# Degrees of a batch as a stream of their own, one batch ahead, in a four-layer graph kernel

## The chip, the cores and the metric

The kernel runs on one core of a Trainium2 chip. A core has a TensorE for matrix products (PE in the profile; PEld is its weight load), VectorE (DVE), ScalarE (ACT), GpSimd (POOL) and SyncE (SP), which here only starts transfers. SBUF is the memory on the core, PSUM holds the results of TensorE, and DMA engines move data between them and the chip's main memory. The metric is the time on the device in microseconds, as the median of several runs.

## The reference

The input is 16 graphs (batches) of 1024 nodes with 128 features and a symmetric 0/1 adjacency of 1024 x 1024. Four residual layers follow one another. The change lies in the second, a three-layer GraphSAGE on a thinned ("dilated") adjacency:

```python
def _sage(x, adj, Wr, Wx, b, mf):
    deg = jnp.clip(jnp.sum(adj, axis=-1, keepdims=True), 1.0, None)
    agg = jnp.einsum('bij,bjd->bid', adj, x) / deg
    out = agg @ Wr + x @ Wx + b
    nrm = jnp.maximum(jnp.linalg.norm(out, axis=-1, keepdims=True), NORM_EPS)
    return out / nrm * mf[..., None]
...
adj_d = _dilate(adj, mask)
h1 = _bn(jax.nn.relu(_sage(x, adj_d, Wr1, Wx1, b1, mf)), g1, be1)
h2 = _bn(jax.nn.relu(_sage(h1, adj_d, Wr2, Wx2, b2, mf)), g2, be2)
h3 = _bn(jax.nn.relu(_sage(h2, adj_d, Wr3, Wx3, b3, mf)), g3, be3)
```

`_bn` takes mean and variance over all batches and nodes, so that every layer must be done with all 16 batches before the next begins. `deg`, the number of neighbours of each node, is the same in the three layers; the kernel computes its reciprocal once, in the first of them, which the code calls layer 1 (`l == 0`).

## The kernel before

The kernel has one stage per part: attention with layer norm, the thinning of the adjacency (to about 990 us), the three GraphSAGE layers, and the last two residual layers. The stage of the change is layer 1, from 990 to about 1350 us. Three names need a word. In the profile the 8-bit adjacency is `carry` (the resident copies of the batches 8 to 15) or `A` (the copies `A8` of the batches 0 to 7, loaded again from main memory, four buffers). `d` stands for both d16 and d8, `step` for the constant matrix of twos.

A batch goes through three generators in the class `Step`, each of which yields where another may take over.

- `first(b)` begins with the degrees: `degree_product` (L1281) multiplies the adjacency by a matrix of twos, 8 blocks times 4 quarters, 32 matmuls, each quarter in a 32-column tile of TensorE's array. ScalarE copies the four quarters of the sums into `row` (L1397, one partition, 2 KB). GpSimd starts a transfer that folds the row into 8 partitions, d16 (L1399). VectorE takes a minimum for a later flag (L1400), halves the sums and clips them at 1 (L1402) and takes reciprocals (L1403). GpSimd writes them to main memory (L1404), and SyncE loads them spread over all 128 partitions as `rdeg` (L1389, 512 KB). Of `row`, d16 and d8 there is one buffer each, of `rdeg` there are three. Then `first` transposes x (L759), splits it into two float32r parts `hi` (ScalarE, L1272) and `lo` (VectorE, L1273, one buffer), widens the adjacency into 8 pieces `a` (ScalarE L1295, VectorE L1293, 8 buffers), multiplies in two halves of 16 matmuls each (L1306) and scales each half by `rdeg` into `ag` (L1416).
- `out(b)` multiplies by the weights (L1432, 16 float32 matmuls, which the profile shows as 32), adds the bias (L1435), squares (L1442), sums (L1443), takes a power on GpSimd (L745) and scales the rows (L1451, L1457).
- `keep(b)` transposes the result (L759), takes statistics (L1471), writes it out (L1474), and already makes layer 2's adjacency product of that batch, with a second split, a second set of pieces and 32 matmuls (L1306), scaled by `rdeg` into `ag` (L1483), which is written out (L1486).

`load(b)` (L1369, L1372) brings A8 and x.

What order do they come in? `take_turns` advances a list of streams one yield at a time. For the i-th of the 16 batches of the layer's order, the list holds `load` of batch i+2, `first` of i+1, `out` of i and `keep` of i-1. I call one round of the list a turn. The framework then arranges the instructions of each engine itself, so the built order differs from the written one. In the built program the degree product stands in two blocks a turn: 20 matmuls after the first 38 of the turn's 64 adjacency matmuls (the 32 of `keep` and the first 6 of the 32 of `first`), where `lo` of `first` is made, and 12 after the last of them. [...]

Of the kernel before, what the change touches and what calls it, by code (L numbers as in the profile page):

```python
# [639 lines left out]
def fast_kernel(ctx: ExitStack, tc: tile.TileContext, t: dict, out: bass.AP, flag: bass.AP):  # L640

    nc = tc.nc
    B, N, D = t["x"].shape
# [110 lines left out]
    def turned(psum, src, tag="h"):  # L754

        for p, c, blocks in halves(psum, tag):
            for i, k in enumerate(blocks):
                s = src[:, k, :] if len(src.shape) == 3 else src[:, k * P:(k + 1) * P]
                nc.tensor.transpose(p[:, i * P:(i + 1) * P], s, identf)  # L759
            yield p, c, slice(blocks[0], blocks[-1] + 1)  # L760
# [50 lines left out]
    def take_turns(streams):  # L811
        while streams:
            streams = [s for s in streams if next(s, streams) is not streams]
# [41 lines left out]
    step = consts.tile([P, P + 512 + P], BF16, name="step")  # L855
# [168 lines left out]
    for b in range(1, B):  # L1024
        streams = []
# [8 lines left out]
    with ExitStack() as ph:  # L1034
# [142 lines left out]
        for i in range(1, len(steps) + 1):  # L1177
            streams = [fixed_point(*steps[i])] if i < len(steps) else []
# [79 lines left out]
    with ExitStack() as ph:  # L1258
# [9 lines left out]
        def split(n):  # L1268

            hi = work.tile([P, NT, P], F32R, name="hi")  # L1270
            lo = work.tile([P, NT, P], F32R, name="lo", bufs=1)
            nc.scalar.copy(hi, n)  # L1272
            nc.vector.tensor_sub(lo, n, hi.bitcast(F32))  # L1273
            return hi, lo

        def degree_product(A):

            acc = ps_a.tile([P, 512], F32, name="acc")
            for jt in range(NT):
                for q in range(4):  # L1280
                    nc.tensor.matmul(acc[32 * q:32 * q + 32, :N // 4], twos[:, :32], A[:, jt, q * N // 4:(q + 1) * N // 4],  # L1281
                                     start=(jt == 0), stop=(jt == NT - 1), tile_position=(0, 32 * q))
            for q in range(4):
                yield acc[32 * q:32 * q + 1, :N // 4], slice(q * N // 4, (q + 1) * N // 4)

        def widened(A):

            for h in range(H2):
                c = slice(h * 512, (h + 1) * 512)
                for i in range(NT // 2):  # L1290
                    a = wide_pool.tile([P, 2, 512], F32R, name="a", bufs=NT)
                    if i % 2:
                        nc.vector.tensor_copy(a, A[:, 2 * i:2 * i + 2, c])  # L1293
                    else:
                        nc.scalar.copy(a, A[:, 2 * i:2 * i + 2, c])  # L1295
                    yield a

        def adjacency_product(pieces, parts):

            for h in range(H2):  # L1300
                acc = ps_a.tile([P, 512], F32, name="acc")
                late = 0 if h else 1
                for i in range(NT // 2 + late):
                    for part, k in zip(parts, (i, i - late)):
                        for jt in range(2 * k, 2 * k + 2) if 0 <= k < NT // 2 else ():
                            nc.tensor.matmul(acc, part[:, jt, :], pieces[h * NT // 2 + k][:, jt - 2 * k, :],  # L1306
                                             start=(part is parts[0] and jt == 0), stop=(part is parts[1] and jt == NT - 1))
                yield acc, slice(h * 512, (h + 1) * 512)
# [6 lines left out]
        class Step:  # L1315
# [73 lines left out]
                nc.sync.dma_start(st.rdeg, bass.AP(tensor=rdeg_d[b].tensor, offset=rdeg_d[b].offset,  # L1389
                                                   ap=[[0, P], [1, N]]))  # L1390

            def first(self, b):

                st = self.batches[b]
                row = work.tile([1, N], F16, name="row", bufs=1)
                for acc, c in degree_product(st.A):
                    nc.scalar.copy(row[:, c], acc)  # L1397
                d16 = small.tile([NT, P], F16, name="d16", bufs=1)
                nc.gpsimd.dma_start(d16, row)  # L1399
                nc.vector.tensor_reduce(nodeg[:NT, b:b + 1], d16, AX.X, OP.min)  # L1400
                d8 = small.tile([NT, P], F32, name="d8", bufs=1)
                nc.vector.tensor_scalar(d8, d16, 0.5, 1.0, op0=OP.mult, op1=OP.max)  # L1402
                nc.vector.reciprocal(d8, d8)  # L1403
                nc.gpsimd.dma_start(rdeg_d[b], d8)  # L1404
                self.load_rdeg(b)
                yield
                st.hT = work.tile([P, N], F32, name="hT")
                for p, c, _ in turned(ps_h, st.x):
                    nc.scalar.copy(st.hT[:, c], p)
                yield  # L1410
                parts = split(st.x)
                pieces = list(widened(st.A))
                yield
                st.ag = work.tile([P, N], F32, name="ag", bufs=3)
                for acc, c in adjacency_product(pieces, parts):
                    nc.vector.tensor_mul(st.ag[:, c], acc, st.rdeg[:, c])  # L1416
                    yield
# [74 lines left out]
        order = [*range(B // 2, B), *range(B // 2)]  # L1492

        lag = 0, 0, 1
        for l in range(3):
            step = Step(l, before)
            if l:
                before.norm()
                step.take_norm()
            if l == 2:  # L1500
                order = [b for pair in zip(order[:B // 2], order[B // 2:]) for b in pair]
            if l == 2:
                take_turns(left)
                left = []
            lead = 0 if l == 1 else 1
            take_turns([step.load(b) for b in order[:1 + lead]])
            if l == 0:
                take_turns([step.first(order[0])])
            outs = [step.out(b) for b in order]
            for i in range(B + lag[l]):  # L1510
                streams, left = left, []
                if i + 1 + lead < B:
                    streams.append(step.load(order[i + 1 + lead]))
                if l == 0 and i + 1 < B:
                    streams.append(step.first(order[i + 1]))
                kept = [step.keep(order[i - 1 - lag[l]])] if i > lag[l] else []
                if l == 2:
                    streams += kept
                if i < B:
                    streams.append(outs[i] if l < 2 else islice(outs[i], 2))  # L1520
                if l == 2 and i:
                    streams.append(outs[i - 1])
                if l < 2:
                    streams += kept
                take_turns(streams)
                if l == 2 and i == 0:

                    wide_ctx.close()
                    l2 = Layers23()
                elif l == 2 and i == B - 4:  # L1530
                    l2.weights(ps_h)
                elif l == 2 and i == B - 3:
                    l2.load(l2.state[0], 0)

            rest = step.keep(order[B - 1])
            next(rest)
            left = [rest]
            before = step
# [7 lines left out]
    with ExitStack() as ph:  # L1546
# [257 lines left out]
        for b in range(B - 1):  # L1804
            streams = []
# [31 lines left out]
def kernel(tc: tile.TileContext, t: dict, out: bass.AP):  # L1837
    nc = tc.nc
    with tc.tile_pool(name="flag", bufs=1) as pool:
        flag = pool.tile([1, 1], I32, name="flag")  # L1840
        fast_kernel(tc, t, out, flag)
        with tc.If(nc.values_load(flag[0:1, 0:1]) != 0):
            general_kernel(tc, t, out)
# [22 lines left out]
```

## Time and profile before

| | |
|---|---|
| Median of 3 runs | 2682.58 us (2681.59 to 2685.39) |
| Profiled execution, its time | 2682.24 us |
| Its span in the profile | 2680.4 us |
| TensorE busy | 2521.3 us, 94% |
| VectorE busy | 2102.6 us, 78% |
| ScalarE busy | 1969.3 us, 73% |
| GpSimd busy | 330.8 us, 12% |

The span is what the profile covers; the time of an execution is a little longer. A row of the timeline has the start, the duration, the engine, the line, the operation with output and inputs, and in brackets the idle time of the engine just before it and what ended it. "<-issue" means that the engine waited for nothing that the profile shows. A row of the waits names the waiting engine and line, what it waited for, and then total, number and longest. In a row of stretches each engine has its busy time and, in brackets, its instructions.

### The profile page before, as it was taken

The numbers are of one execution on the slowest core, as the hardware profiler recorded it, in microseconds if no ns is written. First come the engines' busy times: TensorE is split into PE (matmuls) and PEld (weight loads), VectorE is DVE, ScalarE is ACT, GpSimd is POOL, SyncE is SP. The second block draws the span as 40 slices with busy tenths as digits, with TensorE's granted clock in tenths as the row PEclk, the third lists the DMA queues.
The fourth block names the chain that finished last, engine by engine and source line by source line (L and its number), as shares of the span: only waits on it lengthen the run. The fifth ranks groups of instructions, "written<-read, shape, count | busy, mean of one in ns | idle before, by whom it ended". The sixth has DMA issues, their size and how long they took to land.

```text
span 2680.4 us, 44092 instructions
## 1 busy us (share of the span) xinstructions
PE 2521.3 (94%) x16136; PEld 1800.2 (67%) x16136; DVE 2102.6 (78%) x5830; ACT 1969.3 (73%) x3172; POOL 330.8 (12%) x300
## 2 busy tenths in 40 slices
PE   7999999997889879999999998999999999999986
PEld 5667777765666658887788895466666666666655
DVE  6888888987898867777778875777878787887885
ACT  7898889886888776666555534777777777777773
POOL 0001111103000002111122232001101000001010
PEclk9999999998999989999999998999999999999998
DMA  5555545520000052233366672112221111111100
GB/s 193 181 176 171 173 161 174 179 96 21 2 3 2 1 221 90 100 111 134 133 241 236 211 283 111 40 38 73 74 91 64 64 63 63 63 63 63 48 24 26
DMA packets 109187, 285.59 MB, mean 107 GB/s; under 512 B 12192, under 2 KB 52128, under 8 KB 101792
## 3 DMA queue, kind: packets, MB, share of 16 engines
q1 hardware_dynamic: 87776, 196.58, 21.7%
q0 software_dynamic: 21184, 86.09, 8.8%
q8 instruction: 129, 2.11, 0.3%
q14 instruction: 98, 0.80, 0.1%
HBM read 202.78 MB, written 79.82 MB: 105 GB/s over the span
## 4 chain that ended last, share of the span: by engine, by line
PE 52%; DVE 19%; ACT 11%; issue 8%; POOL 4%; DMA 3%; POOLq 0%; ACTq 0%; DVEq 0%; SPq 0%
PE ph L1618 8%; PE acc L1678 7%; PE acc L1306 7%; PE ph L766 6%; PE ph L1432 4%; PE ph L759 3%; PE pmm L1690 3%; PE acc L973 2%; PE pmm L724 2%; ACT em L985 2%; PE ph L1605 2%; ACT xn L801 2%; DVE mid L1096 2%; DVE keep L1147 2%; POOL ln_rstd L745 2%
## 5 line engine op out<-in xcount | busy, mean ns | idle before, releaser
L973 PEld LDWEIGHTS acc<-hs,em 128*128 128x128 f32 x2048 | 248.7, 192 | 37.9 <-issue 26.8
L973 PE MATMUL acc<-hs,em 128*128 128x128 f32 x2048 | 269.1, 279 | 0.7 <-DVE hs L989 0.3
L1678 PE MATMUL acc<-ex,hs 128*128 128x512 f32 x512 | 248.9, 596 | 7.4 <-DVE hs L1705 4.5
L724 PE MATMUL pmm<-xT,G 128*128 128x512 f32 x512 | 251.4, 604 | 1.4 <-DVE mx L983 0.7
L801 ACT ACTIVATE xn<-xn,ln_nb,ln_rstd 128x128 f32<-128x128 f32 x512 | 204.7, 480 | 55.9 <-DVE ln_nb L799 55.8
L1306 PE MATMUL acc<-a,hi 128*128 128x512 f32 x768 | 233.6, 398 | 11.1 <-DVE a L1293 8.0
L1306 PE MATMUL acc<-a,lo 128*128 128x512 f32 x768 | 229.6, 393 | 5.8 <-DVE lo L1273 5.8
L745 POOL TENSOR_TENSOR ln_rstd<-ln_rstd,mhalf 128x8 f32<-128x8 f32 (+1 forms) x68 | 108.3, 1593 | 969.2 <-DVE ln_rstd L742 513.4
L983 DVE CUSTOM_DVE_ANT_0 em<-pmm,msk 128x1024 f32<-128x1024 f32 x128 | 155.9, 1218 | 35.1 <-PE pmm L724 32.8
L985 ACT ACTIVATE em<-em,mx 128x1024 f32<-128x1024 f32 x128 | 146.0, 1141 | 48.2 <-DVE mx L983 46.5
L1698 ACT ACTIVATE ex<-em,mn 128x1024 f32<-128x1024 f32 x128 | 146.9, 1147 | 45.0 <-DVE mn L1695 44.0
L1690 PE MATMUL pmm<-G,hT 128*128 128x512 f32 (+3 forms) x416 | 175.3, 523 | 0.1
L1695 DVE CUSTOM_DVE_ANT_0 em<-pmm,msk 128x1024 f32<-128x1024 f32 x128 | 155.4, 1214 | 24.5 <-PE pmm L1692 22.3
L1306 PEld LDWEIGHTS acc<-a,hi 128*128 128x128 f32 x768 | 142.2, 189 | 42.4 <-DVE a L1293 10.6
L1306 PEld LDWEIGHTS acc<-a,lo 128*128 128x128 f32 x768 | 143.5, 189 | 40.2 <-DVE lo L1273 10.5
L1156 ACT ACTIVATE carry<-pc,negone 128x1024 fp8e4<-128x1024 f32 x128 | 141.3, 1115 | 26.7 <-PE pc L1155 23.8
L931 ACT ACTIVATE carry<-an 128x1024 fp8e4<-128x1024 f32 x128 | 134.1, 1049 | 23.9 <-DMA an<-in_adj 23.3
L980 ACT ACTIVATE msk<-carry,l0nbig 128x1024 bf16<-128x1024 fp8e4 x128 | 145.9, 1140 | 0.0
L1686 ACT ACTIVATE msk<-A,nbig 128x1024 bf16<-128x1024 fp8e4 x128 | 144.3, 1138 | 0.0
L1618 PE MATMUL ph<-A,hi 128*128 128x512 f32 x512 | 143.2, 420 | 0.8 <-DVE zn L1607 0.6
L1678 PEld LDWEIGHTS acc<-ex,hs 128*128 128x128 f32 x512 | 88.6, 190 | 76.8 <-issue 54.7
L1295 ACT CAST a<-A 128x1024 fp32r<-128x1024 fp8e4 x96 | 98.4, 1048 | 54.5 <-PE acc L1306 53.4
(317 smaller groups left out, 6186.6 us busy)
## 6 DMA issues: line engine op xcount, KB each, us to landing
an<-in_adj SPq DMA_DIRECT2D x128, 512.0 KB, 4.1
adj_d<-carry POOLq DMA_DIRECT2D x16, 1024.0 KB, 4.6
A<-dil_d SPq DMA_DIRECT2D x16, 1024.0 KB, 5.6
rdeg<-rdeg_d SPq DMA_DIRECT2D x32, 512.0 KB, 3.8
A<-adj_d SPq DMA_DIRECT2D x16, 1024.0 KB, 4.8
ag_d<-ag POOLq DMA_DIRECT2D x24, 512.0 KB, 5.4
ag<-ag_d SPq DMA_DIRECT2D x24, 512.0 KB, 5.5
x_d<-xn POOLq DMA_DIRECT2D x16, 512.0 KB, 3.9
```

What stands on the lines that cost most here:

```text
L724: nc.tensor.matmul(p[:, h * 512:(h + 1) * 512], lhsT, rhs[:, h * 512:(h + 1) * 512], start=True, stop=True)
L745: nc.gpsimd.tensor_tensor(r, r, mhalf[:, :n], op=OP.pow)
L766: nc.tensor.matmul(p, W, x[:, c], start=(i == 0), stop=(i == len(pairs) - 1))
L801: nc.scalar.activation(r[:, k.start + i, :], r[:, k.start + i, :], AF.Identity, scale=rstd[:, i:i + 1], bias=nb[:, i:i + 1])
L973: nc.tensor.matmul(s.acc[:, c], em[:, c], hs, start=(jt == 0 and k % 4 == 0), stop=(jt == NT - 1 and k % 4 == 3))
L983: nc.vector.tensor_tensor_reduce(em, e, msk, 1.0, 3.0e38, op0=OP.add, op1=OP.min, accum_out=mn)
L985: nc.scalar.activation(em, em, AF.Exp, scale=-1.0, bias=mn, accum_out=sm)
L1306: nc.tensor.matmul(acc, part[:, jt, :], pieces[h * NT // 2 + k][:, jt - 2 * k, :], start=(part is parts[0] and jt == 0), stop=(part is par ...
L1618: nc.tensor.matmul(p, part[:, jt, :], A[jt][:, c], start=(jt == 0 and i == 0), stop=(jt == NT - 1 and i == 1))
L1678: nc.tensor.matmul(s.acc[:, c], hs, ex[:, c], start=(jt == 0), stop=(jt == NT - 1))
L1690: nc.tensor.matmul(e[:, c], s.hT[:, js], s.G[:, c], start=True, stop=True)
L1695: nc.vector.tensor_tensor_reduce(row, e, msk, 1.0, 0.0, op0=OP.add, op1=OP.min, accum_out=mn)
```

## The change

The degrees leave `first` and become a generator of their own, `degrees`, with two empty yields ahead of the product, one after the row's transfer and one at the end. `first` begins with the load of `rdeg`. Ahead of the loop the degrees of the first two batches are made; in the loop, `degrees` of batch i+2 is the last stream of the turn. The computation is the same.

```diff
-            def first(self, b):
+            def degrees(self, b):
 
                 st = self.batches[b]
+                yield
+                yield
                 row = work.tile([1, N], F16, name="row", bufs=1)
                 for acc, c in degree_product(st.A):
                     nc.scalar.copy(row[:, c], acc)
                 d16 = small.tile([NT, P], F16, name="d16", bufs=1)
                 nc.gpsimd.dma_start(d16, row)
+                yield
                 nc.vector.tensor_reduce(nodeg[:NT, b:b + 1], d16, AX.X, OP.min)
                 d8 = small.tile([NT, P], F32, name="d8", bufs=1)
                 nc.vector.tensor_scalar(d8, d16, 0.5, 1.0, op0=OP.mult, op1=OP.max)
                 nc.vector.reciprocal(d8, d8)
                 nc.gpsimd.dma_start(rdeg_d[b], d8)
+                yield
+
+            def first(self, b):
+
+                st = self.batches[b]
                 self.load_rdeg(b)
                 yield
...
             if l == 0:
-                take_turns([step.first(order[0])])
+                take_turns([chain(step.degrees(order[0]), step.first(order[0])), step.degrees(order[1])])
...
                 if l < 2:
                     streams += kept
+                if l == 0 and i + 2 < B:
+                    streams.append(step.degrees(order[i + 2]))
                 take_turns(streams)
```

In the order of the built program (the profile of before numbers the lines; in the changed file they are up to 10 higher), one turn of TensorE now runs: 16 adjacency matmuls of `keep`, all 32 of the degree product, 4 of `first`, 16 of `keep`, 2 of `first`, 2 of L1432, 7 transposes, 26 of `first`, 14 of L1432, the rest of the transposes. On VectorE, L1400, L1402 and L1403 stand directly ahead of `lo` of `first`; before, they stood among L1435, L1471 and L1443. From layer 2 on, the built order of every engine is the same in both.

## Prediction

> **What bounds the kernel now.** TensorE is busy 94% of the 2680.4 us span, and the change touches one stage only, layer 1 of the three inner graph layers. So I read that stage: busy time over stretches first, then who waits for whom there, then the chain of waits and the timeline of single turns. The stretches are cut at the starts of `keep`'s adjacency product (L1306), one per turn: 1023.58 for the first, 1197.04 for the ninth, 1314.96 for the fourteenth.
>
> ```profile
> core 0: us, PE busy (x) PEld busy (x) DVE busy (x) ACT busy (x) POOL busy (x), PEclk, DMA share, GB/s
> 1023.58:1197.02 173.44, 171.79 (x1155) 142.61 (x1154) 132.17 (x215) 117.58 (x162) 34.35 (x40) 1.00 0.29 102
> 1197.02:1315.22 118.20, 109.23 (x724) 89.04 (x723) 82.49 (x135) 73.77 (x102) 22.40 (x25) 1.00 0.37 131
> ```
>
> Eight turns take 21.68 us each with TensorE 99% busy; the next five take 23.58 with it 92% busy. The clock is 1.00 in both, so the 1.9 us between them is waiting. Who waits (1000 to 1330 us; total, times, longest):
>
> ```profile
> DVE nodeg L1400 <- DMA d<-row: 14.8, 6, 2.7
> ...
> PEld acc L1306 <- DVE a L1293: 10.6, 6, 2.0
> ...
> PEld L1281 <- issue: 9.9, 28, 0.4
> ```
>
> Six times VectorE stands at L1400 until the transfer of the degree row lands, and six times TensorE waits for a widened piece `a` that VectorE makes later. The timeline of the ninth turn has both (`d` is d16 and d8, `A` is the copy A8):
>
> ```profile
> 1193.85 0.32 SPq L1369 DMA_DIRECT2D A<-dil_d  x1
> ...
> 1194.17 0.51 POOL L1399 DMA_DIRECT2D d<-row  x1 [6.55 <-ACT row L1397]
> ...
> 1198.85 0.27 DVE L1400 TENSOR_REDUCE nodeg<-d 8x1 f32<-8x128 f16 x1 [2.43 <-DMA d<-row]
> ...
> 1201.96 0.69 DVE L1293 CAST a<-A 128x1024 fp32r<-128x1024 fp8e4 x1
> ...
> 1202.70 0.76 PEld L1306 LDWEIGHTS acc<-a,hi 128*128 128x128 f32 x4 [1.72 <-DVE a L1293]
> ```
>
> The 2 KB row goes out 0.3 us after a load of 1 MB and lands 4.66 us later; in the undisturbed turns it lands in 1.6 us (median of eight). [...] statistics, row sums and pieces stand behind. The chain of waits gives the prices of an undisturbed turn:
>
> ```profile
> 1003.79 0.99 PE acc L1281 x32
> ...
> 1105.02 3.77 PE ph L1432 x32
> 1108.79 1.77 PE ph L759 x16
> 1110.55 8.21 PE acc L1306 x36
> 1118.79 1.24 DVE lo L1273
> 1120.07 6.19 PE acc L1306 x26
> ```
>
> There TensorE is the bound, but for one VectorE operation (`lo`, one buffer) that no matmul covers entirely.
>
> [...] The degree product is the only one of this stage in 32-column tiles, and the trace shows 0.35 us of "issue" idleness ahead of it, 28 times for 9.9 us.
>
> **The change, part by part.** The instructions are the same, so the count costs nothing; only places change. I took the places from the order of the built program.
>
> 1. *Row transfer and L1400 to L1403.* The product for the batch after next now runs after the first half of `keep`'s adjacency product, its row goes out while no large load starts, and L1400 stands after the row scaling (L1457), ahead of `lo` of `first`. Call the start of `keep`'s product s. A load of A8 still starts when `keep` has read the old copy, near s, and needs 4.8 us (its median). The row: 16 matmuls at 0.228 (8.21/36) are 3.65, the product 0.99, four ScalarE copies 1.49, 0.3 to GpSimd's issue: s+6.5. So the load has landed. The row should land in 1.6 us. This removes the wait of 1.9 us in five turns (9.5) and in a sixth after 1314.96 (1.9): 11.4 us. What is late next? TensorE, as in the first eight turns.
>
> 2. *VectorE's new place.* L1400, L1402 and L1403 take 1.4 us ahead of `lo`. From the end of the degree product: copies, issue and landing are 0.1+1.5+0.3+1.6 = 3.5, the three 1.4, `lo` 1.23: done at 6.15. TensorE has by then 22 adjacency matmuls (5.0), then two of L1432's (0.45) and seven transposes (0.75) as cover: 6.2. It just fits. Queued behind the three are `lo`, one piece and the scaling of `keep`'s second half; TensorE waits for `lo` alone. If the row is later, each microsecond is one for TensorE, in every turn. I take 0.1.
>
> 3. *TensorE's order.* The 32 matmuls of L1281 stood in two blocks, 20 of them under `lo`, 12 before L1432. Now they are one block, and L1432's two and seven transposes cover `lo`. Sum of a turn: 64 x 0.228 + 3.77 + 1.77 + 0.99 = 21.1. Splitting L1432 may add up to 0.3 (a start of L1432 after L1281 idles 0.2 now). I take 21.35, bounds 21.1 and 21.68. Thirteen turns: 13 x (21.68 - 21.35) = 4.3 us.
>
> 4. *The head.* The product of the second batch moves to before the first adjacency product, where TensorE sits idle 2.60 us for `hi`; 0.99 less on the path later. Against it, `lo` now stands ahead of the first scaling (L1416), until TensorE has read the old `lo` at 1003.8; scaling then ends near 1005.7, as TensorE, with transposes and 13 degree matmuls as cover, arrives. GpSimd's second row goes ahead of the first rdeg write: 0.5 us, unneeded until 1005. I take a gain of 0.7, bounds -0.5 and 1.5.
>
> 5. *Other queues.* GpSimd's order is now row, rdeg write, ag write, hT write, power; the power is no longer behind the rdeg write. SyncE's rdeg load no longer waits for a fresh write, only for its buffer (3 of them, freed by L1483), a turn ahead: nothing. The product needs A8 a batch earlier: that load starts near the start of one `keep` product and is read 3.65 us into the next, a turn of 21 us for 4.8: hidden. If that cover were gone, TensorE would wait 4.8 - 3.65 = 1.2 us in four turns. Layers 2 and 3 keep their order.
>
> Sum: 11.4 + 4.3 + 0.7 = 16.4 us. The profiled execution took 2682.24 us (span 2680.4), the median is 2682.58; from the first I get 2665.8, on the median's scale 2666.2.
>
> **Rivals.**
> - *Only the stall goes.* The turn stays at 21.68, because splitting L1432 or the tight `lo` eats what one block saves. For: 0.05 us of margin in point 2. Against: 0.35 us of issue idleness is one time fewer. Gain 11.4 + 0.7 = 12.1: 2670.5.
> - *The wait moves to `lo` in part.* The row lands 0.6 us later because the hT write (512 KB) shares the engines with A8's load: turns of 21.95, gain 11.4 - 3.5 + 0.7 = 8.6: 2674.
> - *Slower.* The row lands in 4.66 us in every turn, as it did in the six: `lo` ends 3.0 late, and TensorE waits 3 us thirteen times: 39 - 16.4 = 22.6 slower, 2705. It decides from 1.3 us of lateness per turn (16.4/13), that is, a landing of 3 us. Against: no large transfer starts between s+0.1 and the row's issue.
> - *No effect.* The piece `a` is late for another reason (row scaling waits for GpSimd's power, 1.55 us in that turn), so TensorE still waits in those six turns: gain of 5 at most, 2678 or above.
> - *More.* Turns at 21.1: gain 11.4 + 7.5 + 1.5 = 20.4: 2662.
>
> **How the numbers follow.** Forecast 0.55 (2664 to 2668.5), only the stall 0.22, `lo` in part 0.08, more 0.05, no effect 0.06, slower 0.04. The range 2661 to 2675.5 takes in the first four nearly whole and leaves out the last two and the tails. About 0.2% (5.4 us) is what a measurement of this kernel can tell from no change: faster 0.90, same 0.06, slower 0.04.
>
> **What would show it.** Right: VectorE standing at the row sum for tenths only, no wait of L1306 for `a`, turns of 21.2 to 21.5 us throughout from 1023 on, L1281 preceded by one idle 0.35 a turn. Wrong: L1306 waiting for `lo` by over 0.3 us a turn (point 2), L1281 waiting for A8's load (point 5), L1432 waiting for `ag` at the head (point 4), or a row landing above 2 us.

## The result, and the profile after

The changed kernel takes 2666.47 us (median of 6 runs, 2666.07 to 2668.35) beside 2682.09 for the kernel before on the same chip: ratio 0.9941, 95% interval 0.9931 to 0.9952, 15.6 us less. 2666.2 was forecast. Line numbers from 1397 on have moved: the row's transfer is L1401, the three degree instructions on VectorE are L1403, L1405 and L1406, `out`'s product is L1440, the scalings L1424 and L1491.

The same cuts through both traces show where the 15.0 us between the spans (2680.4 and 2665.4) are:

| Stretch (us) | before | after | gained | forecast |
|---|---|---|---|---|
| up to the first adjacency product | 993.80 | 992.43 | 1.4 | none |
| head, to `keep`'s first product | 29.78 | 27.71 | 2.1 | 0.7 |
| thirteen turns | 291.38 | 281.98 | 9.4 | 13.8 |
| tail of layer 1 | 38.27 | 35.87 | 2.4 | 1.9 |
| layers 2, 3 and the rest | 1327.17 | 1327.41 | -0.2 | none |

The first row is no effect of the change: over the eleven traces of this study that point lies anywhere from 992.3 to 997.4 us. So layer 1 gained 13.9 us where 16.4 was forecast: the turns missed by 4.4, head and tail made good 1.9 of it, and the 1.4 us of the first row, which bring the sum nearer to the forecast, are luck. The stretches of the trace after, cut at nearly the same places of a turn (TensorE, its weight load, VectorE, ScalarE, GpSimd, clock, DMA share, GB/s):

```profile
core 0: us, PE busy (x) PEld busy (x) DVE busy (x) ACT busy (x) POOL busy (x), PEclk, DMA share, GB/s
1020.14:1192.90 172.76, 170.93 (x1152) 143.58 (x1150) 131.35 (x216) 119.50 (x160) 31.67 (x40) 1.00 0.29 99
1192.90:1302.12 109.22, 107.56 (x726) 90.28 (x725) 83.28 (x138) 75.42 (x103) 19.62 (x26) 1.00 0.44 140
1107.70:1129.05 21.35, 21.34 (x147) 17.97 (x145) 16.50 (x28) 14.97 (x22) 3.83 (x6) 1.00 0.29 100
1064.99:1088.19 23.20, 21.56 (x145) 17.96 (x144) 16.61 (x28) 14.92 (x21) 4.10 (x5) 1.00 0.26 91
```

The last five turns now cost about as little as the first eight (21.8 and 21.6 us each, late rows included), though more is transferred in them (DMA share 0.44). The third line is one undisturbed turn, 21.35 us with TensorE busy all the time. The fourth is one of three turns that the forecast did not have. They are longer, by 1.9, 0.4 and 1.9 us. The waits (1000 to 1330 us; total, times, longest):

```profile
PEld L1281 <- issue: 4.7, 14, 0.4
PEld acc L1306 <- DVE lo L1273: 4.3, 4, 1.9
...
DVE nodeg L1403 <- DMA d<-row: 4.0, 3, 1.9
```

TensorE no longer waits for a piece `a`. The idleness ahead of L1281 comes 14 times instead of 28. But VectorE still stands at the row three times, and what waits behind it is `lo`, not `a`. First a good turn, the ninth, in the timeline:

```profile
1192.90 0.32 SPq L1369 DMA_DIRECT2D A<-dil_d  x1
...
1199.98 0.56 POOL L1401 DMA_DIRECT2D d<-row  x1 [2.81 <-ACT row L1399]
...
1201.75 0.27 DVE L1403 TENSOR_REDUCE nodeg<-d 8x1 f32<-8x128 f16 x1
...
1203.06 1.15 DVE L1273 TENSOR_TENSOR lo<-n,hi 128x1024 fp32r<-128x1024 f32 x1
...
1204.34 0.70 PE L1306 MATMUL acc<-a,lo 128*128 128x512 f32 x2
```

The megabyte starts 7.1 us ahead of the row instead of 0.3. L1403 and TensorE's first use of `lo` have no bracket: neither waited, and `lo` ends 0.13 us before TensorE takes it. Then the chain of waits through a bad turn and the next good one:

```profile
1069.58 3.70 DMA d<-row
1073.28 0.02 issue
1073.30 0.27 DVE nodeg L1403
1073.58 0.14 DVE d L1405
...
1074.61 1.16 DVE lo L1273
...
1075.82 6.21 PE acc L1306 x26
...
1090.01 0.99 PE acc L1281 x32
1090.99 5.23 PE acc L1306 x22
1096.23 0.44 PE ph L1440 x4
1096.67 0.77 PE ph L759 x7
1097.44 5.94 PE acc L1306 x26
1103.37 3.12 PE ph L1440 x28
```

In the good turn the chain is TensorE from end to end and `lo` is gone from it. In the bad one the row took 3.70 instead of 1.6 us with no A8 load near. L1403 began 0.02 us after it had landed, and `lo`, which stands behind the three degree instructions in VectorE's built order, 1.33 us after. So 2.1 us of lateness made 1.9 us of TensorE's time.

### The profile page after: what moved, and what is told of

It reads as the page before. It is cut to its first block, busy times and chain, and to the rows that moved or that the text cites. A ratio compares the mean times of both kernels' runs of the same rounds, so it can differ in the third digit from the quotient of the medians.

```text
span 2665.4 us, 44084 instructions
## 1 busy us (share of the span) xinstructions
PE 2513.8 (94%) x16132; PEld 1801.1 (68%) x16136; DVE 2102.3 (79%) x5830; ACT 1972.8 (74%) x3172; POOL 325.2 (12%) x300
## 4 chain that ended last, share of the span: by engine, by line
PE 58%; DVE 18%; ACT 10%; issue 5%; POOL 4%; DMA 2%; POOLq 0%; ACTq 0%; DVEq 0%; SPq 0%
PE acc L1306 11%; PE ph L1628 8%; PE acc L1688 7%; PE ph L766 6%; PE ph L1440 5%; PE ph L759 4%; PE pmm L1700 3%; PE acc L973 2%; PE pmm L724 2%; PE ph L1615 2%; ACT em L985 2%; ACT xn L801 2%; DVE mid L1096 2%; DVE keep L1147 2%; DVE em L983 2%
## 5 line engine op out<-in xcount | busy, mean ns | idle before, releaser
L1295 ACT CAST a<-carry 128x1024 fp32r<-128x1024 fp8e4 x96 | 98.8, 1047 | 43.1 <-PE acc L1306 42.9
```

## Experiments

All are compared with the kernel before on their own chip. "Layer 1" is the time in the profile from the first adjacency product to the end of the layer (before 359.4, after 345.6), which leaves out the drift of earlier stages.

| Kernel | median, us | before on that chip | ratio (95%) | layer 1 |
|---|---|---|---|---|
| after_again | 2666.73 | 2684.02 | 0.9938 (0.9926 to 0.9949) | 345.2 |
| e17_all_loads | 2671.16 | 2683.07 | 0.9958 (0.9945 to 0.9972) | 348.2 |
| e14_behind_lo | 2673.09 | 2684.02 | 0.9952 (0.9940 to 0.9965) | 347.6 |
| e3_two_hops | 2674.86 | 2683.91 | 0.9970 (0.9959 to 0.9982) | 349.1 |
| e5_head_undone | 2675.05 | 2683.91 | 0.9969 (0.9959 to 0.9978) | 350.1 |
| e6_two_blocks | 2677.71 | 2683.91 | 0.9975 (0.9968 to 0.9983) | 354.6 |
| e1_load_pool | 2680.03 | 2683.91 | 0.9981 (0.9974 to 0.9987) | 355.5 |
| e13_clock | 2686.76 | 2684.02 | 1.0005 (0.9995 to 1.0015) | 360.1 |
| e4_not_ahead | 2688.52 | 2684.02 | 1.0018 (1.0010 to 1.0026) | 364.4 |

**Is the A8 load the cause of the six stalls?** Theory: yes. Rival: the row was late for another reason. The kernel before, with that load behind the row:

```diff
-nc.sync.dma_start(st.A.bitcast(F32), dil8_d[b])
+(nc.gpsimd if self.l == 0 and b >= 4 else nc.sync).dma_start(st.A.bitcast(F32), dil8_d[b])
```

> The kernel before, with one edit: in layer 1 the 1 MB load of A8 is issued by GpSimd, where the order written for that queue puts it behind the row's DMA, and no longer by SyncE, where it starts 0.3 us ahead of the row. TensorE's order stays that of before (degree product in blocks of 20 and 12). Theory (the row is late because the A8 load is ahead of it): the row lands in 1.6 us in every turn, the six stalls of 1.9 us go, the turns stay at 21.68 us: 2682.1 - 11.4 = 2670.7 us, ratio 0.9957. Rival (the row of those turns is late for another reason, or the load starts close enough behind it to hold it up all the same): the row still takes 4.7 us in six turns, 2682 us. Rival (the load is now late for its use): above 2685 us, with a wait of L1293 or L1281 for the A8 load.

Layer 1 gained 3.9 us, a third of what was expected. Four of the six stalls went, and the turns there are 21.68 to 21.72 us. The two that stayed are those whose A8 load belongs to layer 2, which the edit left on SyncE. One turn of each kind, in the timeline:

```profile
1192.77 0.51 POOL L1399 DMA_DIRECT2D d<-row  x1 [7.06 <-ACT row L1397]
1193.36 0.58 POOL L1369 DMA_DIRECT2D A<-dil_d  x1
1194.93 0.26 DVE L1400 TENSOR_REDUCE nodeg<-d 8x1 f32<-8x128 f16 x1
...
1279.23 0.32 SPq L1369 DMA_DIRECT2D A<-dil_d  x1
1279.57 0.52 POOL L1399 DMA_DIRECT2D d<-row  x1 [7.06 <-ACT row L1397]
1284.28 0.28 DVE L1400 TENSOR_REDUCE nodeg<-d 8x1 f32<-8x128 f16 x1 [2.46 <-DMA d<-row]
1288.14 0.73 PE L1306 MATMUL acc<-a,hi 128*128 128x512 f32 x2 [1.34 <-DVE a L1293]
```

With the load 0.6 us behind the row, L1400 begins 2.2 us after the row's issue and has not waited for it; with the load 0.3 us ahead of the row, L1400 begins 4.7 us after the issue and has waited 2.46 us. The expectation had counted six where the edit reached four; the last stall even grew to 3.3 us. So the edit was widened to the first two loads of layer 2 (`self.l == 1 and b < 2` as well):

> The kernel before, with the six A8 loads that lie at a row in its trace all issued by GpSimd behind the row: the four of layer 1 that the run e1_load_pool moved, and the first two of layer 2, which that run had left on SyncE and whose two turns kept their stall. Theory (the load ahead of the row is what makes it late): no turn has a row over 2 us unless something else is ahead of it, no stall of 1.3 us for `a` with 0.5 us for `lo`; the last row may still be late by the 512 KB load of hT that starts at the same moment. The span of layer 1 falls from 359.4 us by 6 x 1.9 = 11.4 us to 348 us, or to 350 us if the last stall stays; time 2671 to 2673 us, ratio 0.9955 to 0.9963. Rival (the two late rows of that run had another cause): they stay, layer 1 takes 352 us or more.

Every row from the fourth on landed in 1.5 to 1.6 us, no stall was left, and layer 1 took 348.2 us, 11.2 less than before against 11.4 worked out. One of the turns that had stalled, and the five turns from the ninth on as one stretch (TensorE busy 99% of it):

```profile
1194.93 0.51 POOL L1399 DMA_DIRECT2D d<-row  x1 [6.57 <-ACT row L1397]
1195.52 0.58 POOL L1369 DMA_DIRECT2D A<-dil_d  x1
1197.09 0.26 DVE L1400 TENSOR_REDUCE nodeg<-d 8x1 f32<-8x128 f16 x1
...
1197.80:1306.30 108.50, 107.48 (x724) 89.15 (x722) 82.89 (x136) 73.51 (x102) 23.74 (x30) 1.00 0.40 141
```

This settles the first term of the sum, with TensorE's order still that of before: the turns stayed at 21.70 us.

**Does the number of blocks make the 0.33 us per turn?** The changed kernel, with a yield in the middle of the product, so that other work comes between its halves (`degrees` passes the yield on):

```diff
                 for jt in range(NT):
...
+                if jt == 3:
+                    yield None
```

> The changed kernel, with the degree product given out in two halves of 16 matmuls with other streams' work between them, where the changed kernel has one block of 32. Theory (each entry into and exit from the 32-column form costs TensorE some 0.3 us beside the matmuls): an undisturbed turn takes 21.7 instead of 21.35 us; 13 x 0.35 = 4.5 us more, 2671.0 us, ratio 0.9959; if the other order of VectorE lets late rows pass, up to 4 us of it come back, but the undisturbed turn still shows 21.7. Rival (the 0.33 us a turn between the two kernels comes from where the block lies, at a join that has no other wait, and not from their number): undisturbed turn 21.35, 2666.5 us or less.

The waits show the idleness ahead of L1281 28 times again:

```profile
PEld L1281 <- issue: 9.7, 28, 0.4
```

A turn in which TensorE waits for nothing behind the row takes 21.86 us: 0.51 more, where 0.35 was expected. (Rows take 2.6 us and more in nearly all these turns. In four of them TensorE waited 0.6 to 1.3 us for a scaling behind the row.) How much of the 0.51 us is the second block? In the traces of before, after and this run the last adjacency matmul ahead of the product starts 0.32 us before it, where adjacency matmuls follow one another in 0.23, and the next matmul starts 0.20 us behind the product's last. By these starts the product takes 1.5 us of TensorE's time in two blocks and 1.3 in one. So the number of blocks counts, and not only the place, as the rival had it; but the other 0.3 us lie elsewhere in an order that the edit also changed (the 16 transposes stand in one row again). Nor is the block all of the 0.33 us between the two kernels: by the same starts, `lo` held up TensorE by 0.28 us in each turn of before, which is gone, while the step from an adjacency matmul to the transposes inside `keep`'s product, 0.48 us, gives back about as much.

**Is the lead of a batch needed, or only the one block?** The degrees in the turn of their own pieces again, in one chain ahead of `first`, the product still one block. The two empty yields go as well, and the head has no second product:

```diff
-    streams.append(step.first(order[i + 1]))
+    streams.append(chain(step.degrees(order[i + 1]), step.first(order[i + 1])))
...
-    streams.append(step.degrees(order[i + 2]))
```

> The changed kernel, with a batch's degrees in the same turn as its pieces again, ahead of them in one chain: nothing runs a batch ahead, but the degree product stays one block of 32 matmuls, between the adjacency product and the output product. Theory (what counts is the number of blocks and what stands behind the row on VectorE, not the batch of lead): turns of 21.35 us, no stall of 1.9 us in six turns; with the head of the kernel before and without its second product 2669 us, ratio 0.995. Rival (the lead matters: the reciprocal row has to be written, read back and used within the same turn): waits of L1421 for the reciprocal row, and of L1437 behind them, turns over 22 us, 2675 us or more.

This version is slower than the kernel before, and the reason is not the rival's: no wait for the reciprocal row. TensorE's own work did shrink (21.38 us busy in a turn of 22.07), but its order left `lo` uncovered, 0.7 us a turn, and from the ninth turn on the A8 load stood ahead of the row again, now with `lo` behind it:

```profile
1196.89 0.32 SPq L1369 DMA_DIRECT2D A<-dil_d  x1
1197.22 0.51 POOL L1399 DMA_DIRECT2D d<-row  x1 [6.54 <-ACT row L1397]
1201.84 0.27 DVE L1401 TENSOR_REDUCE nodeg<-d 8x1 f32<-8x128 f16 x1 [1.83 <-DMA d<-row]
...
1211.90 0.74 PE L1306 MATMUL acc<-a,lo 128*128 128x512 f32 x2 [2.37 <-DVE lo L1273]
```

So one block did not help in this order. In the changed kernel the row stands 7 us away from the load and `lo` has its cover; whether that place in the order could be had without the lead, no run shows.

**What delays the three rows?** In each of the three turns, and in none of the other ten, the queues show a packet of queue q8 or q14 within the row's time. The profile calls these queues "instruction"; I read such a packet as a fetch of the program itself. The row is 32 small packets of queue q0. The queue table of the changed kernel from 1070.6 to 1071.0, 1071 to 1072 and 1072 to 1073 us, the late row (packets, MB, share of 16 engines):

```profile
q0 software_dynamic: 30, 0.00, 5.2%
...
q8 instruction: 1, 0.02, 6.0%
...
q0 software_dynamic: 2, 0.00, 0.3%
```

Thirty packets pass, then one packet of 16 KB, which takes 0.96 us (6.0% of what 16 engines have in 1 us), then the last two. In the row of the turn before, all 32 pass within 0.4 us. In the late one the fetch's packet began only 0.4 us behind the thirtieth, so the last two were late by then; that part is not explained. The changed kernel once more, as it is:

> The changed kernel once more, unchanged, on the chip of the other runs. Theory (a row lands late when the fetch of the next piece of the program, a DMA of 8 or 16 KB, runs at the same moment; the program is the same, so the fetches fall at the same places): the same three turns of the thirteen (the third, the sixth and the eleventh of those between the second block of 32 and the end) are longer, by 1.9, 0.4 and 1.9 us, each with a fetch in the row's window, and no other. Rival (chance meetings with other transfers): late rows in other turns, without a fetch. Time: ratio 0.9941 to the kernel before.

The same three turns were late, the third, sixth and eleventh (23.09, 22.03 and 22.56 us), with rows of 3.5, 2.5 and 3.0 us and a fetch in each; their stalls:

```profile
1079.19 0.73 PE L1306 MATMUL acc<-a,lo 128*128 128x512 f32 x2 [1.48 <-DVE lo L1273]
...
1143.92 0.73 PE L1306 MATMUL acc<-a,lo 128*128 128x512 f32 x2 [0.42 <-DVE lo L1273]
...
1251.90 0.74 PE L1306 MATMUL acc<-a,lo 128*128 128x512 f32 x2 [0.96 <-DVE lo L1273]
```

In all six late rows of the two traces the last two packets begin within 0.02 us of the fetch's end. No run takes the fetch alone away, but in e5_head_undone, below, the sixth turn's row met none and landed in 1.6 us. So the same program had the three meetings in the same turns twice, and the rows took 3.7, 2.2 and 3.7 us the first time, 3.5, 2.5 and 3.0 the second. Can TensorE be spared it? Two versions put the degree instructions behind `lo`: the first by taking the row through main memory in two transfers, with which the built order has them there,

```diff
-                nc.gpsimd.dma_start(d16, row)
+                nc.gpsimd.dma_start(row_d[b], row)
+                nc.gpsimd.dma_start(d16, row_d[b].rearrange("o (t p) -> (o t) p", p=P))
```

> The changed kernel, with the row going through main memory in two DMAs, so that VectorE's three degree instructions stand behind both `lo` of a turn and two of its scalings, and a late row has nothing of TensorE's queued behind it. Theory (in the changed kernel the 4.4 us beyond thirteen turns of 21.35 us are three late rows that hold up `lo`): all thirteen turns take 21.35 us, 277.6 us in sum, no wait of L1306 for `lo` behind a row: 2666.5 - 4.4 = 2662.1 us, ratio to the kernel before 0.9926. Rival (the late rows only mark moments in which main memory is busy, and TensorE would stand for something else): 2666.5 us, with the same turns at 22 to 23 us. Rival (the second transfer makes the reciprocal row late for the next turn's scalings, or three more instructions in front of a scaling cost): 2670 us or more, with a wait of L1426 or L1493.

the second by two tiny instructions that read `lo` (`self.lo`), for all batches but the first two of the order:

```diff
+nc.vector.tensor_scalar(d8[:, 0:1], self.lo[:NT, 0, 0:1].bitcast(F32), 0.0, None, op0=OP.mult)
+nc.vector.tensor_scalar(nodeg[:NT, b:b + 1], self.lo[:NT, 0, 0:1].bitcast(F32), 0.0, None, op0=OP.mult)
 nc.vector.tensor_reduce(nodeg[:NT, b:b + 1], d16, AX.X, OP.min)
```

> The changed kernel, with VectorE's three degree instructions of a turn put behind `lo` by two tiny VectorE instructions that read a piece of `lo` and write a place which the degree instructions then overwrite. Unlike the run with two transfers, the row takes one transfer and the head stays that of the changed kernel. Theory: no stall of TensorE behind a late row (4.4 us less over thirteen turns), and the 0.24 us a turn that the planner's other split of the turning matmuls (4 and 8 where the changed kernel has 7 and 5) cost in that run (3.1 us more): 2666.5 - 1.3 = 2665.2 us, ratio 0.9936. Rival (two more instructions and a later reciprocal row cost more than the late rows): 2668 us or more, with waits of L1496 or L1429 for the reciprocal row.

In both, no steady turn is late any more: 21.6 us each. In the second, the row of the sixth turn still lands in 2.2 us beside a fetch and costs nothing; in the third and the eleventh turn the fetch came just behind the row, so that a row of 3 us and more was not put to the test. In the third turn, the queue table from 1074.9 to 1075.5 and from 1075.5 to 1076.5 us shows

```profile
q0 software_dynamic: 32, 0.00, 3.7%
...
q8 instruction: 1, 0.02, 6.5%
```

and the row took 1.6 us: here its 32 packets had all begun before the fetch's. Neither version is faster than the changed kernel. The built order now covered `lo` with 4 transposes instead of 7, and each turn took 0.24 us more than 21.35, 3.1 us in sum: where the first run's expectation had 21.35, this ate most of the 4.4 us. Beyond the turns, the second lost 3.3 us at the end of the layer, where a scaling stood 1.5 us for a buffer that a write still read (the clock fell behind that, 0.51 from 1345 to 1350 us, but there the next layer has begun):

```profile
1342.91 0.69 DVE L1496 TENSOR_TENSOR ag<-acc,rdeg 128x512 f32<-128x512 f32 x1 [1.54 <-DMA ag_d<-ag]
```

The first lost it in the head (2.8 us for L1426). So 1.3 us was to be had in the turns and was had there, 1.3 us (259.1 us for twelve turns beside 260.4), but the whole got longer. Nothing tried beats the changed kernel.

**Where do the 2.1 us of the head come from?** In the changed kernel TensorE's granted clock is 1.00 when the first adjacency product starts at 992.43 us, and the stretch ahead of it shows some work:

```profile
988.43:992.43 4.00, 1.26 (x12) 0.79 (x9) 0.02 (x1) 3.94 (x8) 0.52 (x1) 1.00 0.01 1
992.43:997.63 5.20, 5.20 (x23) 4.31 (x24) 3.94 (x7) 5.17 (x10) 1.13 (x2) 1.00 0.01 1
```

In the kernel before, the clock was 0.50 there and the first 32 matmuls, from 993.80 us on, took 9.92 instead of 7.4 us:

```profile
988.80:992.21 3.41, 1.39 (x15) 0.84 (x8) 0.91 (x2) 3.38 (x7) 0.06 (x1) 1.00 0.00 0
992.21:999.04 6.83, 5.24 (x12) 4.13 (x13) 3.05 (x5) 4.60 (x6) 0.96 (x2) 0.50 0.01 1
```

The second batch's degrees put back at the start of the first turn:

```diff
-take_turns([chain(step.degrees(order[0]), step.first(order[0])), step.degrees(order[1])])
+take_turns([chain(step.degrees(order[0]), step.first(order[0]))])
...
-streams.append(step.first(order[i + 1]))
+streams.append(chain(step.degrees(order[1]), step.first(order[1])) if i == 0 else step.first(order[i + 1]))
```

> The changed kernel, with the second batch's degrees back at the start of the first turn, as in the kernel before, instead of beside the first batch's. The steady turns stay those of the changed kernel. Theory (the head gained because the additional product kept TensorE's clock at full speed when the first adjacency product began): the first 32 adjacency matmuls run at a granted clock of 0.5 again for some 5 us and take 9.9 instead of 7.4 us; the head with the turn after it is 2.1 us longer: 2668.6 us, ratio 0.9950. Rival (the head gained by leaving out waits, and the clock follows something else): the clock stays at 1.00 from 992 us on, and the time is 2666.5 us or less, since the scaling of the head is no longer behind the second trio (-0.6).

```profile
989.98:993.98 4.00, 0.66 (x4) 0.42 (x5) 0.02 (x1) 3.94 (x8) 0.53 (x1) 0.79 0.01 1
993.98:999.18 5.20, 5.20 (x12) 4.12 (x13) 2.99 (x5) 3.03 (x4) 0.50 (x1) 0.51 0.01 1
```

The clock is 0.51 again, as theorised: 12 matmuls instead of 23 in 5.2 us. All eleven traces divide in this way: from 990 to 1000 us the clock is 1.00 in the six with the second product at that place, and 0.65 or 0.66 in the mean in the five without, as much as 0.50 for 6.8 us. The head and first turn lost 6.0 us rather than 2.1, since two batches' degrees now stood in one turn: TensorE waited 3.05 us for the second scaling, and the clock fell once more behind that wait (0.80 and 0.86 from 1020 to 1030 us). The clock by itself, in the kernel before, with a second product whose result is thrown away:

```diff
-take_turns([step.first(order[0])])
+take_turns([step.first(order[0]), idle(step.batches[order[1]].A)])
```

> The kernel before, with a second degree product in the head whose result is thrown away (four single elements of it are copied to a scrap tile): nothing else is moved. It adds work and serves only to keep TensorE busier from 984 to 990 us. Theory (the granted clock in the head follows what TensorE did in the microseconds ahead of it): clock 1.00 instead of 0.50 in the first 5.2 us of the first adjacency product, whose first 32 matmuls take 7.4 instead of 9.9 us; all else as in the kernel before: 2682.1 - 2.5 = 2679.6 us, ratio 0.9991. Rival (the clock was raised by something else in the changed kernel): clock 0.50 as before, 2682 us, or more by the added product.

```profile
996.76:1001.96 5.20, 5.20 (x23) 4.31 (x24) 3.88 (x6) 4.62 (x10) 0.50 (x1) 1.00 0.02 4
...
1295.00:1300.00 5.00, 3.12 (x12) 2.27 (x11) 3.73 (x8) 1.39 (x2) 2.25 (x2) 0.90 0.14 48
1300.00:1305.00 5.00, 5.00 (x18) 3.83 (x17) 3.49 (x7) 2.07 (x3) 0.29 (x1) 0.76 0.29 90
```

The first line is the theory's: clock 1.00, first 32 matmuls in 7.5 us. The head took 27.9 us, 1.9 less than before, so that the clock alone makes most of the 2.1. The time of the whole did not fall with it. The profile shows 0.6 us given back in the next product and 1.7 us at 1295 to 1305 (worked out from the two clocks, 0.90 and 0.76, over 5 us each), where the lower clock followed a stall of 1.9 us behind a late row; why the median of thirteen runs is not below that of before stays open.

## Why the prediction was right, point by point

The sum is nearer than its parts: the medians lie 15.6 us apart where 16.4 was forecast, but layer 1, which alone the change touches, gained 13.9 us in the profiles, with misses on both sides.

1. *Row wait: right, by cause and size.* e17_all_loads removes it alone and gains 11.2 us in layer 1, against 11.4. The rival "no effect" (the piece `a` late because of GpSimd's power) falls with it.
2. *VectorE's new place: the step that failed.* "It just fits" was right for an undisturbed turn (0.13 us to spare, 0.05 worked out), and so was "If the row is later, each microsecond is one for TensorE". Wrong was "I take 0.1", which rested on a row of 1.6 us in every turn. The prediction reckoned with large transfers of the kernel alone; in the changed order a fetch of the program met the row in three turns and cost 4.2 us. Such fetches are in the queue table of before too, but its trace could not show the price: the one that met an undisturbed row there (issued at 1020.89 us) ended 0.6 us behind the row's issue, and that row took 1.69 us.
3. *TensorE's order: right.* 21.35 us a turn was forecast and measured. Of its parts, e6_two_blocks shows that one block fewer pays, some 0.2 us; the forecast also had `lo` covered and something lost by splitting, and the starts of the matmuls show both. The idleness ahead of L1281 was halved with the block (9.9 to 4.7 us).
4. *The head: right sign, wrong reason and size.* 0.7 was taken, 2.1 came. The waits went the other way: TensorE stood 0.63 us for L1424 and 0.50 us at the transposes behind it. What paid was the clock, some 2.5 us in the first 32 matmuls: 9.92 us in the kernel before, with the clock at 0.50 up to 999.04 us, and 7.4 in the changed one at 1.00. How much work ahead of the product is enough, the traces do not say. The 4 us ahead of it held 0.66 us of work in e5_head_undone, where the clock fell, and 1.26 in the changed kernel, where it did not; but in the kernel before it fell 1.6 us ahead of the product, and the 3.4 us ahead of that held 1.39. The prediction read the 2.60 us of idleness in the head as room and left the clock there out.
5. *Other queues: right.* No wait for A8; its load takes 6.0 us (median) beside the hT write instead of 4.8 and still has a turn. In the tail 2.4 us came where 1.9 was expected.

The rival "slower" named the right mechanism: e4_not_ahead has rows of 4.4 to 5.3 us with `lo` behind them and loses to the kernel before. The changed kernel escapes it by 7 us of distance between load and row, not by being insensitive.

## What to carry to other kernels

When a tiny transfer decides a wait, ask what is on the DMA engines ahead of it, the program's own fetches included (here a megabyte issued 0.3 us ahead went with a row of 4.66 us, a fetch of 16 KB with rows of 3.0 to 3.7, and without them it was 1.6), and keep behind its waiting instruction only what has cover. A stream that runs a batch ahead pays here mainly by its distance to a large load: with the loads put behind the row and no lead, 11.2 of the 13.9 us of layer 1 came as well. Both together were not tried. And behind a gap in TensorE's work, look at its clock: with 2.60 us of idleness ahead of the first adjacency product in both, it was 0.50 for 6.83 us in the kernel before and 1.00 in the changed one.

## What the runs showed of the hardware that I had not expected

- A fetch of 16 KB of program (q8) shows as one packet, 0.96 us long in the third turn of the changed kernel. In the four late rows that met one, the last two of the row's 32 packets began as it ended: 3.0 to 3.7 us instead of 1.6. In the two that met a fetch of 8 KB (q14) it was 2.2 and 2.5.
- One wait of TensorE of 1.9 to 3.3 us was followed by a lower clock in four of these kernels (e1_load_pool, e3_two_hops, e5_head_undone, e13_clock): 0.67 to 0.90 as a mean of 5 us, as much as half the clock for 3.4 us. By these means it cost up to 1.7 us more, an estimate. It didn't follow each time: six waits of 2.4 to 3.1 us in e4_not_ahead left the clock at 1.00, and so did the six shorter stalls of the kernel before (1.2 to 1.5 us).
- A megabyte issued 0.3 to 0.6 us ahead of the 2 KB row made it land in 4.4 to 4.7 us in the kernel before; issued 0.5 to 0.6 us behind it (e17_all_loads), it left the row at 1.5 to 1.6.
